# Two more tiles' own rows in the second phases, logits inside the second layer, one expert computed on all rows

## The chip, the core and the metric

The kernel runs on one core of a Trainium2 chip. The core has a matrix engine (TensorE, PE in the profile, with its weight loads as PEld), a vector engine (DVE), a scalar engine (ACT), GpSimd (POOL, which here mostly issues gathers) and a queue engine (SP, which here issues plain transfers). Each engine runs its own instructions strictly in its own order and waits on semaphores for the others. The metric is the device time of one execution in microseconds (us). Three runs of the kernel before took 981.47, 988.24 and 991.53 us; the median is 988.24.

## What is computed

1250 nodes with 512 features and 20000 edges. Two graph layers with a maximum over neighbours, then a feed-forward layer in which each of eight experts chooses 512 rows:

```
x = x + gnn(layernorm(x))          # two layers, each: relu(segment_max(x[src], dst) @ W_rel.T + b + x @ W_root.T)
y = layernorm(x)
probs = softmax(y @ Wr, axis=0)    # [N, 8], softmax over the rows
vals, idx = top_k(probs.T, 512)    # every expert picks 512 rows
h = gelu(y[idx] @ W1 + b1)         # [8, 512, 256]
x = x.at[idx].add(vals * (h @ W2 + b2))
```

All of it is in float32 to the outside.

## The kernel before, in words

Rows are held in ten tiles of 125 nodes (`acc` holds the running maximum of each tile, 512 wide). `fast_gnn` (line 42) does the two layers, `expert_choice` (line 1121) the rest. A wrapper (`InOrder`, line 24) pins every instruction of `fast_gnn` to the order in which the program writes it, and puts it on one line of the profile, L34. In `expert_choice` the engines are called without the wrapper, and the scheduler may interleave instructions of different steps.

The sources of a node are taken in three ways. Up to two sources per block of 125 source rows are picked by **blocks**: 100 steps per layer (`block_steps`, line 557), each six one-hot matmuls of 512 columns into `pq`, then one `tensor_max` of 1024 columns on DVE into `acc2`. Seven further sources per node are its **own rows** (`own`, line 451): seven gathers per tile by `nat_i`, in groups of four and three, merged on DVE (`merged`, `joined`). What is left over is **late rows** (`late_groups`, line 646): 107 gathers per layer, in 30 groups, for nodes sorted by how much they have left; their result goes to a table in memory (`late_d`, in the profile `ovf_d`) and is fetched back by one gather per tile (`backs`). A group's buffer is `hb`, of which there are four, and POOL issues every gather.

Each layer has two phases. `first_phase` (line 586) runs the blocks, spreads the merges of the gathered groups evenly between them (`due`), and lays the root product (`root_part`, line 290: four transposes, a bias matmul and four matmuls with `wroot`, stored in `root_d`) between them too. In layer 0 the own rows of tiles 0 to 2 come before the phase (`KEPT`), and those of tiles 3 to 5 at its end; in layer 1 those of tiles 0 to 5 (`EARLY = 6`). The gathers of a group are written, and so issued, ahead of the blocks that precede its merge.

`second_phase` (line 701) does the own rows that are left (tiles 6 to 9, `own_rest`), fetches the late rows back for four, four and two tiles, and finishes the tiles in order: `turn` transposes a tile, `conv` (line 670) multiplies it by `wrel` and adds the root row that SP has fetched into `ahead`, and `finish` is `hidden` in layer 0 (relu, store to the next layer's table, split in three bf16 parts by `parts`) and `residual` in layer 1 (fetch the row of x, add, moments, normalise, store to `y_d`, transpose into `yT`). A `finish` is a generator: its next stage runs when the next tile ends, so that three or four tiles are under way. `yT` lies in the memory of the one-hots (`ohs`), which are dead by then.

`expert_choice` loads the router's weights, multiplies them with `yT` in three chunks (line 1185; each router column is repeated over 16 partitions, which search different bounds at once), takes the exponent over the rows (line 1193), searches the bar of the 512th value in eight rounds of a 1250-wide count on DVE and a small matmul (lines 1233 to 1249), numbers the chosen rows by scans (1256 to 1264), adds the bias product of the experts to all rows and stores them (1268 to 1273), and turns the numbers into row lists by one-hot matmuls (`listed`, line 1295). Then each expert gathers its 512 rows (`gathered`), transposes them, multiplies by `w1` (line 1335), applies gelu, multiplies by `w2` (line 1342), scales (1345) and adds its rows to the output by indirect transfers (1346).

Of the kernel before, what the change touches and what calls it, by code (L numbers as in the profile page):

```python
# [9 lines left out]
F32 = mybir.dt.float32  # L10
# [8 lines left out]
P = 128  # L19
# [22 lines left out]
def fast_gnn(tc, ctx, sh, io, y_d):  # L42

# [223 lines left out]
    def parts(t, row, last):  # L267

        act.copy(xh[:TN, t, 0, :], row)
        yield  # L270
        dve.tensor_sub(row, row, xh[:TN, t, 0, :])
        act.copy(xh[:TN, t, 1, :], row)
        yield
        last.tensor_sub(xh[:TN, t, 2, :], row, xh[:TN, t, 1, :])
        yield
# [13 lines left out]

    def root_part(layer, t):  # L290
# [4 lines left out]
        fetch_row(layer, t + 3)  # L295
# [20 lines left out]
    def begin_rows(t0, t1):  # L316
        inverted(t0, t1)
        for t in range(t0, t1):
            normed(t, acc[:TN, t, :])
            stored(table_d[0][t * BR:t * BR + BN, :], acc[:, t, :])  # L320
            split[t] = parts(t, acc[:TN, t, :], pool)
            next(split[t])
# [134 lines left out]
    EARLY = 6  # L457
# [122 lines left out]
    ROOT_PIECES = 2 + KC  # L580

# [4 lines left out]
    def first_phase(layer, lead, groups, lists, blocks, done):  # L586
# [20 lines left out]
        for n, (rows, i, fresh, whole) in enumerate(groups):  # L607
            due = lead + (n_steps - lead) * n // len(groups)
# [54 lines left out]
    ahead = {}  # L663

    def fetch_root(layer, t):
        if t < NT:
            ahead[t] = rl = gk.tile([P, D], F32, name="ahead", bufs=4)
            sp.dma_start(rl[:TN], root_d[layer][t * TN:(t + 1) * TN, :])

# [7 lines left out]
    def hidden(t, pm):  # L677
# [4 lines left out]
        yield from parts(t, row[:TN], dve)  # L682

    def residual(t, pm):
# [13 lines left out]
        turned(yn[:TN], yT[:, :, t * TN:(t + 1) * TN])  # L698
        yield

    def second_phase(layer, finish, beside):
# [36 lines left out]
        for t in range(3):  # L738
            fetch_root(layer, t)
        order = list(range(EARLY, NT))  # L740
        own_rest(order[0])
        backs((0, 1, 2, 3))
        ready = (0, 1, 2, 3)
        ended(0, 1)
        own_rest(order[1])
        ended(2, 3)
        backs((4, 5, 6, 7))
        ready = (4, 5, 6, 7)
        ended(4, 5)
        own_rest(order[2])  # L750
        ended(6, 7)
        own_rest(order[3])
# [4 lines left out]
        while going:  # L757
            on()

    pbad = ps_m.tile([P, D], F32, name="pm")  # L760
    pe.matmul(pbad[:1, :1], bads, ones_col, start=True, stop=True)
    dve.tensor_scalar(flag_i, pbad[:1, :1], 1.0, None, op0=ALU.min)
    first_phase(0, 6, late_groups(0) + own_groups(0, range(KEPT, EARLY)), set(),
                block_steps(set(range(KEPT))), 0)
    load_root(1)
# [3 lines left out]
    def begun():  # L769
        for _ in range(2 * ready_steps):  # L770
            next(blocks)
# [4 lines left out]
    first_phase(1, 10, late_groups(1) + own_groups(1, range(EARLY)), set(range(NT)), blocks, ready_steps)  # L776
    second_phase(1, residual, lambda: None)
    gctx.close()
    return acc, yT, flag_i
# [341 lines left out]
def expert_choice(tc, ctx, sh, xs, yT, y_d, out):  # L1121
# [3 lines left out]
    ident, node_tile, rows = sh["ident"], sh["TN"], sh["rows"]  # L1125
    wr, fw1, fb1_t, fw2, fb2 = sh["wr"], sh["fw1"], sh["fb1_t"], sh["fw2"], sh["fb2"]
# [4 lines left out]
    TN = node_tile  # L1131
    NT = len(rows)
    CAP = min(512, N)
    R = P // E
    chunks = []
    step = (N + 2) // 3
    for c0 in range(0, N, step):
        chunks.append((c0, min(step, N - c0)))
    rp = ctx.enter_context(tc.tile_pool(name="route", bufs=1))
    rp2 = ctx.enter_context(tc.tile_pool(name="route2", bufs=2))  # L1140
    fwp = ctx.enter_context(tc.tile_pool(name="fwp", bufs=2))
    ps_t = ctx.enter_context(tc.tile_pool(name="fps_t", bufs=2, space=PSUM))
    ps_m = ctx.enter_context(tc.tile_pool(name="fps_m", bufs=3, space=PSUM))
    ps_x = ctx.enter_context(tc.tile_pool(name="ps_x", bufs=1, space=PSUM))


    wr_s = rp.tile([P, KC, E], F32, name="wr_s")
    nc.sync.dma_start(wr_s, wr.rearrange("(c p) e -> p c e", p=P))
    wr_rep = rp.tile([P, KC, E, R], F32, name="wr_rep")
    for c in range(KC):  # L1150
        nc.gpsimd.tensor_copy(wr_rep[:, c], wr_s[:, c].unsqueeze(2).to_broadcast([P, E, R]))
    alike = rp.tile([P, P], F32, name="alike")
    nc.gpsimd.memset(alike, 1.0)
    alike_v = alike.rearrange("p (e r) -> p e r", r=R)
# [317 lines left out]
```

## Time and profile before

The profiled execution took 982.43 us by itself; its span from the first to the last instruction is 980.7 us, at a mean granted PE clock of 0.905. It lies 5.8 us under the median of the three runs. All stage times below are of that execution.

| stage | from to (us) | length |
|---|---|---|
| loading, normalising, lists of sources | 0 to 128 | 128 |
| first phase, layer 0 | 128 to 350 | 222 |
| second phase, layer 0 | 350 to 431.5 | 81 |
| first phase, layer 1 | 431.5 to 652 | 221 |
| second phase, layer 1 | 652 to 742 | 90 |
| logits, exponent | 742 to 758.6 | 16 |
| search of the bar | 758.6 to 783.7 | 25 |
| scans, lists, first gathers | 783.7 to 830.5 | 47 |
| eight experts | 830.5 to 962 | 132 |
| last additions and end | 962 to 980.7 | 19 |

| engine | busy us | share of the span |
|---|---|---|
| PE | 685.5 | 70% |
| DVE | 668.2 | 68% |
| POOL | 527.9 | 54% |
| ACT | 143.6 | 15% |

How to read it: an engine's busy time says little about the end, because the stages have different limits. What counts is the last wait to end in each stage. In a line of the timeline the first two numbers are the start and the length, then come engine, source line, operation, output and inputs, how many instructions are merged, and in brackets how long the engine had been idle and what released it.

### The profile page before, as it was taken

What the parts mean: (1) busy time and instruction counts of PE and PEld (TensorE: products, weight loads), DVE (VectorE), ACT (ScalarE), POOL (GpSimd) and SP (SyncE); (2) the same over time, 40 slices, a digit from 0 to 9 for tenths busy, and PEclk for the clock granted to TensorE, in tenths of its full rate; (3) what the DMA queues carried; (4) which work ended last, traced back from release to release, by engine and by line L of the source; (5) the groups of instructions that cost most, each with busy time, mean ns of one, the idle gap of its engine ahead of it and who ended that gap; (6) DMA issues with size and microseconds to landing.
All of it is one profiled execution on the core that took longest, in us unless ns stands there. A gap on an engine that the chain in (4) does not pass through costs nothing.

```text
span 980.7 us, 8205 instructions
## 1 busy us (share of the span) xinstructions
PE 685.5 (70%) x2367; PEld 362.0 (37%) x2367; DVE 668.2 (68%) x1248; ACT 143.6 (15%) x259; POOL 527.9 (54%) x528
## 2 busy tenths in 40 slices
PE   0000527888989859879888898866875255999992
PEld 0000314444545424435444454432433223454440
DVE  6799649899998854728998998983543775232211
ACT  0700000000100003320000010000322001222210
POOL 6743667766667664037777777775300003464642
PEclk9999968899999979979999999987987565999996
DMA  7438477967767675337977887666623004688863
GB/s 197 124 104 235 120 213 182 220 201 213 236 208 231 178 234 196 109 114 218 205 242 219 262 261 229 203 197 213 221 82 120 1 26 167 143 200 173 192 105 46
DMA packets 71001, 172.63 MB, mean 176 GB/s; under 512 B 12887, under 2 KB 17557, under 8 KB 70947
## 3 DMA queue, kind: packets, MB, share of 16 engines
q0 software_dynamic: 38368, 116.29, 44.5%
q1 hardware_dynamic: 31598, 54.60, 17.7%
q10 hardware_dynamic: 980, 1.12, 0.5%
q8 instruction: 21, 0.34, 0.1%
q14 instruction: 34, 0.27, 0.1%
HBM read 142.48 MB, written 29.45 MB: 175 GB/s over the span
## 4 chain that ended last, share of the span: by engine, by line
PE 27%; DVE 23%; DMA 22%; POOL 12%; issue 10%; ACT 3%; SPq 1%; ACTq 0%; DVEq 0%; POOLq 0%
POOL hb L34 10%; DMA hb<-table_d,late_i 10%; PE pm L34 6%; PE pm L1335 6%; DVE acc L34 6%; PE pm L1342 5%; PE pq L34 4%; DMA line<-in_x 4%; DVE wide L34 4%; DVE hb L34 4%; DMA ahead<-root_d 2%; DVE keys L34 1%; DMA pl_i<-in_dst 1%; DMA hb<-table_d,nat_i 1%; PE pt L1329 1%
## 5 line engine op out<-in xcount | busy, mean ns | idle before, releaser
L34 PE MATMUL pq<-xh,ohs 126*125 126x512 bf16 x1200 | 297.2, 391 | 75.5 <-DVE acc L34 72.9
L34 POOL DMA_INDIRECT hb<-table_d,late_i x214 | 226.2, 1057 | 115.3 <-issue 51.7
L34 PEld LDWEIGHTS <-ohs 126*125 126x125 bf16 x1200 | 165.8, 140 | 228.5 <-issue 156.5
L34 DVE TENSOR_TENSOR acc<-acc,pq 125x1024 f32<-125x1024 f32 x180 | 219.1, 1217 | 42.6 <-PE pq L34 35.2
L34 POOL DMA_INDIRECT hb<-table_d,nat_i x140 | 147.7, 1055 | 94.4 <-issue 34.8
L34 PE MATMUL pm<-wrel,turn 128*125 128x512 f32 x160 | 82.6, 664 | 12.2 <-DVE acc L34 11.6
L1315 POOL DMA_INDIRECT ysel<-y_d,idx x32 | 30.9, 965 | 111.2 <-PE pi L1300 72.5
L34 PE MATMUL pm<-wroot,turn 128*125 128x512 f32 x160 | 87.0, 626 | 0.0
L34 ACT COPY acc<-pq 125x1024 f32<-125x1024 f32 x20 | 20.2, 1012 | 380.9 <-PE pq L34 362.7
L34 DVE TENSOR_TENSOR wide<-wide,hb 125x1024 f32<-125x1024 f32 (+1 forms) x60 | 71.4, 1190 | 1.9
L1345 DVE TENSOR_SCALAR oo<-pm,val 128x512 f32<-128x512 f32 x32 | 24.0, 751 | 62.7 <-PE pm L1342 62.7
L1346 POOL DMA_INDIRECT out<-oo,idx x32 | 50.3, 1573 | 28.0 <-DVE oo L1345 19.8
L1335 PE MATMUL pm<-yselT,w 128*128 128x512 f32 x128 | 58.0, 607 | 1.2 <-ACT yselT L1330 1.0
L1342 PE MATMUL pm<-w,hT 128*128 128x512 f32 x128 | 57.7, 599 | 0.0
L34 DVE TENSOR_TENSOR hb<-hb 125x1024 f32<-125x1024 f32 (+2 forms) x55 | 52.6, 957 | 2.3 <-DMA hb<-table_d,late_i 2.1
L34 DVE TENSOR_TENSOR wide<-hb 125x1024 f32<-125x1024 f32 (+1 forms) x40 | 48.0, 1200 | 6.6 <-DMA hb<-table_d,late_i 6.4
L34 PEld LDWEIGHTS pm<-wrel,turn 128*125 128x125 f32 x160 | 32.5, 213 | 51.5 <-issue 48.0
L34 PE MATMUL pt<-ident,loc 125*20 125x125 f32 x10 | 3.3, 386 | 61.1 <-DVE loc L34 60.7
L34 PEld LDWEIGHTS pm<-wroot,turn 128*125 128x125 f32 x160 | 32.5, 204 | 11.5 <-issue 3.1
L1342 PEld LDWEIGHTS pm<-w,hT 128*128 128x128 f32 x128 | 23.7, 190 | 32.8 <-issue 26.8
L1335 PEld LDWEIGHTS pm<-yselT,w 128*128 128x128 f32 x128 | 24.2, 194 | 29.7 <-issue 27.4
L34 POOL DMA_INDIRECT hb<-ovf_d,slot_i x20 | 19.6, 978 | 24.7 <-DVE wide L34 19.5
(222 smaller groups left out, 700.2 us busy)
## 6 DMA issues: line engine op xcount, KB each, us to landing
w<-in_fw SPq DMA_DIRECT2D x16, 512.0 KB
ohs<-idx_d SPq DMA_DIRECT2D x10, 615.2 KB
ahead<-table_d SPq DMA_DIRECT2D x20, 250.0 KB
root_d<-line SPq DMA_DIRECT2D x20, 250.0 KB
ahead<-root_d SPq DMA_DIRECT2D x20, 250.0 KB
ovf_d<-line SPq DMA_DIRECT2D x18, 224.0 KB
hb<-table_d,late_i POOLq DMA_INDIRECT x214, 6.0
line<-in_x SPq DMA_DIRECT2D x10, 250.0 KB
```

Source lines behind the costliest of these rows:

```text
L34: made = call(*args, **kwargs)
L1315: nc.gpsimd.indirect_dma_start(out=ysel[:, c, :], out_offset=None, in_=y_d[:, :], in_offset=bass.IndirectOffsetOnAxis(ap=idx[:, c:c + 1], ...
L1329: nc.tensor.transpose(pt[:, k, :], ysel[:, c, k * P:(k + 1) * P], ident)
L1335: nc.tensor.matmul(ph[:, :CAP], w1[:, k, f * P:(f + 1) * P], yselT[:, k, :], start=(k == 0), stop=(k == KC - 1))
L1342: nc.tensor.matmul(po, hT[:, f, c * P:(c + 1) * P], w2[:, f, :], start=(f == 0), stop=(f == FC - 1))
L1345: nc.vector.tensor_scalar_mul(oo, po, val[:, c:c + 1])
L1346: add = nc.gpsimd.indirect_dma_start(out=out[:, :], out_offset=bass.IndirectOffsetOnAxis(ap=idx[:, c:c + 1], axis=0), in_=oo[:, :], in_off ...
```

## The change

**Tiles.** `EARLY` goes from 6 to 4: the own rows of tiles 4 and 5 leave both first phases and go to the second phases, whose order is written out anew. `BEFORE = 4` lets four more blocks run ahead of the first merge in both first phases. The small matmul for the flag (`pbad`) moves behind the first phase of layer 0. The load of layer 1's root weights moves from before the second phase of layer 0 to just before its last two tiles. The root rows of tiles 0 to 2 are fetched from `root_part` (tiles 7 to 9) and no longer at the start of the second phase. `parts` gets a second row to write the difference to, instead of writing over the row that is being stored.

**Head.** A new function `routing_head` is called between the first and second phase of layer 1. Its small tensors and the weights of expert 0 lie in the unused rest of `ohs`. In the order of the program it puts twelve transfers on SP (the router's weights, `w1` and `w2` of expert 0 with 512 KB each, biases), and on POOL the masks, index rows and the repeated router weights, all ahead of the second phase's gathers and rows. `residual` gets a fifth stage that computes the logits of its tile, with a copy on ACT and a maximum on DVE.

**Experts.** `expert_choice` is now pinned to program order too. Expert 0 is computed on all 1250 rows (`dense_steps`: 24 matmuls of 417 columns, 20 of 512, in pieces placed between the rounds of the search and after it), and is added to the rows with a gate that is zero where the row was not chosen. The other seven experts go on as before, with three weight buffers instead of two; the list of expert e+1 is made before the work of expert e.

```diff
-    def parts(t, row, last):
+    def parts(t, row, r1, last):
         act.copy(xh[:TN, t, 0, :], row)
         yield
-        dve.tensor_sub(row, row, xh[:TN, t, 0, :])
-        act.copy(xh[:TN, t, 1, :], row)
+        dve.tensor_sub(r1, row, xh[:TN, t, 0, :])
+        act.copy(xh[:TN, t, 1, :], r1)
...
     def root_part(layer, t):
-        fetch_row(layer, t + 3)
+        if t + 3 < NT:
+            fetch_row(layer, t + 3)
+        else:
+            fetch_root(layer, t + 3 - NT)
...
-    EARLY = 6
+    EARLY = 4
+    BEFORE = 4
...
-            due = lead + (n_steps - lead) * n // len(groups)
+            due = lead + BEFORE + (n_steps - lead - BEFORE) * n // len(groups)
...
     def residual(t, pm):
...
         turned(yn[:TN], yT[:, :, t * TN:(t + 1) * TN])
         yield
+        head["logits"](t, ps_q.tile([P, R, D], F32, name="pq")[:, 0, :])
+        yield
...
-        for t in range(3):
-            fetch_root(layer, t)
-        order = list(range(EARLY, NT))
-        own_rest(order[0])
+        own_rest(4)
         backs((0, 1, 2, 3))
+        own_rest(5)
         ended(0, 1)
-        own_rest(order[1])
+        own_rest(6)
         ended(2, 3)
         backs((4, 5, 6, 7))
+        own_rest(7)
         ended(4, 5)
-        own_rest(order[2])
+        own_rest(8)
         ended(6, 7)
-        own_rest(order[3])
+        own_rest(9)
         beside()
         backs((8, 9))
         ended(8, 9)
...
-    load_root(1)
     def begun():
+        load_root(1)
         for _ in range(2 * ready_steps):
             next(blocks)
...
+    spare = ohs.rearrange("p t n -> p (t n)").bitcast(F32)[:, KC * N:]
+    head = routing_head(tc, sh, spare, yT)
     second_phase(1, residual, lambda: None)
...
+def routing_head(tc, sh, spare, yT):
+    sp.dma_start(wr_s, wr.rearrange("(c p) e -> p c e", p=P))
+    for e in range(DENSE):
+        sp.dma_start(w1, fw1[e].rearrange("(c p) f -> p c f", p=P))
+        sp.dma_start(w2, fw2[e].rearrange("(c p) d -> p c d", p=P))
+    sp.dma_start(fb1_s, fb1_t)
+    for e in range(E):
+        sp.dma_start(fb2_s[e * R:e * R + 1, :], fb2[e:e + 1, :])
...
+    for c in range(KC):
+        pool.tensor_copy(wr_rep[:, c], wr_s[:, c].unsqueeze(2).to_broadcast([P, E, R]))
+    def logits(t, pl):
+        for c in range(KC):
+            pe.matmul(pl[:, :r], wr_rep[:, c].rearrange("p e r -> p (e r)"),
+                      yT[:, c, t * TN:t * TN + r], start=(c == 0), stop=(c == KC - 1))
+        act.copy(prob[:, t * TN:t * TN + r], pl[:, :r])
+        dve.reduce_max(tops[:, t:t + 1], prob[:, t * TN:t * TN + r], axis=AX.X)
...
 def expert_choice(tc, ctx, sh, xs, yT, y_d, out, head):
+    def dense_steps():
+        for e in range(DENSE):
+            for c0, w in chunks:
+                for f in range(FC):
+                    for k in range(KC):
+                        pe.matmul(ph[:, :w], w1[:, k, f * P:(f + 1) * P], yT[:, k, c0:c0 + w], ...)
+                        if k % 2:
+                            yield
+                    act.activation(hT[f][:, c0:c0 + w], ph[:, :w], AF.Gelu, ...)
+            for t in range(NT):
+                for f in range(FC):
+                    pe.matmul(po[:r], hT[f][:, t * TN:t * TN + r], w2[:, f, :], ...)
+                act.copy(res[e][:r, t, :], po[:r])
+                yield
+    dve.reduce_max(sm[:, 0:1], head["tops"], axis=AX.X)
+    act.activation(prob, prob, AF.Exp, bias=sm[:, 1:2], accum_out=sm[:, 2:3])
+    beside(2)
...
         pe.matmul(pn, alike, sat, start=True, stop=True)
+        if i == 0:
+            by_token(prob, pcol)
+        else:
+            beside()
...
+    beside(9)
     by_token(place, at)
+    beside(4)
...
+    def own_row(t):
+        pe.matmul(po[:r], chosen[:, t * TN:t * TN + r], fb2_s, start=True, stop=True)
+        dve.tensor_add(xs[:r, t, :], xs[:r, t, :], po[:r])
+        for e in range(DENSE):
+            dve.scalar_tensor_tensor(xs[:r, t, :], res[e][:r, t, :], gate[:r, t, e:e + 1], xs[:r, t, :], ...)
+        sp.dma_start(out[t * TN:t * TN + r, :], xs[:r, t, :])
...
+    made = listed(DENSE)
+    ysel = gathered(made[0])
+    for _ in steps:
+        pass
+    for t in range(NT):
+        own_row(t)
+    for e in range(DENSE, E):
+        work = expert(e, *made, ysel)
+        if e + 1 < E:
+            nxt = listed(e + 1)
+            ysel_n = gathered(nxt[0])
+        next(work)
+        next(work)
```

## The prediction

> **What bounds the kernel now.** I read the table of windows by stage first, because every stage has its own limit, then the timeline around each boundary, then the waits. Columns: window, length, busy time (instructions) of PE, PE's weight loads, DVE, ACT, POOL, then PE's granted clock, DMA share, GB/s.
>
> ```profile
> 128.00:352.00 224.00, 180.11 (x682) 98.73 (x681) 199.70 (x236) 19.28 (x28) 150.34 (x145) 0.92 0.72 206
> 352.00:431.00 79.00, 63.36 (x176) 30.71 (x176) 38.68 (x51) 23.29 (x40) 22.90 (x23) 0.90 0.49 158
> 431.00:652.00 221.00, 186.78 (x704) 101.89 (x704) 193.94 (x184) 20.46 (x30) 171.34 (x160) 0.95 0.78 227
> 652.00:742.00 90.00, 62.07 (x180) 30.98 (x180) 45.15 (x109) 19.59 (x40) 29.20 (x35) 0.84 0.53 172
> 742.00:759.00 17.00, 10.57 (x25) 5.57 (x26) 4.25 (x16) 3.32 (x8) 0.99 (x4) 0.80 0.40 129
> 759.00:784.00 25.00, 8.16 (x26) 6.09 (x25) 18.63 (x60) 1.65 (x10) 0.00 (x0) 0.50 0.00 1
> 784.00:830.00 46.00, 22.41 (x88) 13.72 (x89) 32.85 (x91) 3.59 (x14) 7.68 (x8) 0.61 0.29 99
> 830.00:962.00 132.00, 129.41 (x408) 62.37 (x406) 33.13 (x88) 28.12 (x46) 70.65 (x55) 0.99 0.72 154
> ```
>
> The first phases are DVE's (199.7 of 224 us, 193.9 of 221), with PE at 180 to 187. The second phases are no engine's: PE 62 of 90, DVE 45, POOL 29; they are waits. The search leaves PE idle, and the experts are PE's (129.4 of 132).
>
> The timeline shows which waits (start, length, engine, operation, in brackets the idle time before it and what ended it):
>
> ```profile
> 138.98 1.23 DVE L34 TENSOR_TENSOR wide<-hb 125x1024 f32<-125x1024 f32 x1 [5.72 <-DMA hb<-table_d,late_i]
> ...
> 367.39 1.12 PE L34 MATMUL pm<-ahead,ident 125*125 125x512 f32 x2 [4.30 <-DMA ahead<-root_d]
> ...
> 431.49 0.94 POOL L34 DMA_INDIRECT hb<-table_d,late_i  x1 [30.80 <-DVE line L34]
> ...
> 654.51 1.43 SPq L34 DMA_DIRECT2D line<-in_x  x1
> ...
> 677.97 0.69 DVE L34 SCALAR_TENSOR_TENSOR acc<-pm,line 125x512 f32<-125x512 f32 x1 [18.85 <-DMA line<-in_x]
> ...
> 744.07 10.28 PE L1185 MATMUL pm<-ohs,wr_rep 128*128 128x417 f32 x24 [2.52 <-POOL wr_rep L1151]
> ...
> 744.31 1.28 ACT L1193 ACT_TABLE_LOAD   x1 [2.15 <-DMA fb_s<-in_fb]
> ...
> 947.94 7.13 PE L1335 MATMUL pm<-yselT,w 128*128 128x512 f32 x16 [0.68 <-ACT yselT L1330]
> ```
>
> Read from these: the first merge of layer 0 waits 5.7 us for a gather; POOL stands still for 30.8 us of the second phase of layer 0; in layer 1 the row of `x` issued at 654.51 is used only at 677.97: SP moved about 1.0 MB in 25.8 us (39.7 GB/s) while POOL issued a 250 KB gather every 1.25 us (200 GB/s).
>
> **The change part by part**, as time after less time before.
>
> (a) First phase, layer 0: **-10**. An own tile's merges are five DVE operations, 1.22 + 0.69 + 1.23 + 0.69 + 0.69 = 4.5 us; two tiles, 9.0. Four more blocks ahead fill some 3 of the 5.7 us (a block is six matmuls, 1.4 us on PE, and 1.22 on DVE). PE, 180 us with a further wait behind each block, gives 2 back. Bounds: -15 (9.0 + 5.7, all paid) to -5.
>
> (b) Second phase, layer 0: **-5**. Added: 14 gathers at 0.95 + 0.30 us on POOL, 17.5 us, under its 30.8 us idle, and 9.0 us of DVE, which is busy 38.7 of 79. Gone: the 4.3 us wait for the first root row, and the waits of the in-place subtraction for the store of the same row (DVE waits 25.2 us in seven places for `table_d<-line`, most of them hidden). What is late next is the gathers. Bounds: -9 (4.3 + one uncovered wait of about 5) to +4 (half of the merges uncovered).
>
> (c) First phase, layer 1: **-8**. Again 9.0 of DVE, and 14 gathers less (about 19 of POOL's 171). No wait stands at its start to be filled; PE, at 187 of 221, keeps 1. Bounds: -15 (POOL's relief paid too, where its buffers hold blocks up) to -2 (PE and the gathers already bind).
>
> (d) Second phase, layer 1: **+21**. In the changed order the four copies of the repeated router weights stand on POOL ahead of all gathers of this phase and wait for SP's transfer of `wr`, which stands behind the last store of `root_d`, at the phase's start. Before, 11 gathers (own rows of tile 6, four late ones) were issued in the 15 us ahead of it. The same transfer and copies took 2.2 + 1.0 us at 741.58 to 744.7, so the first gather is issued some 3.4 us into the phase. Tile 4's product needs the 29th gather (7 + 4 + 7 + 7 + 4): 3.4 + 29 x 1.25 + 6.3 for landing (as for the late rows before) + 4 for merge, transposes and copy = 50 us into the phase; before it began at 692.3, 40.1 in: +10. From there on each tile's step gets four logits matmuls (10.28 us for 1250 rows, 1.03 a tile), a copy on ACT (0.58) and a maximum on DVE, which stands ahead of the addition that frees the next product's PSUM; DVE's merges (4.5) come into the same step. Steps were 5.3 to 6.7 us apart undisturbed; I take 7.9. Tile 4's product to the last copy of `yT`: 5 x 7.9 + 12.5 (as before, 729.7 to 742.2) + three logits stages with nothing beside them (1.03 + 0.58 + 0.25 + four handovers of 0.35 = 3.3 each) = 62, against 49.9: +12, of which I count 11. Bounds: +12 (steps at 6.7, half the drain hidden) to +28 (steps at 9).
>
> (e) From the last copy of `yT` to the search: **-9**. Before, 16.4 us: transfer, copies, 10.28 of matmuls, exponent. After: one tile's logits 1.9, handovers 1, maximum over tiles 0.5, and the exponent with its table load, 4: 7.4. Before, the table load (1.28 us at 744.31) ran under the matmuls; in the changed order it follows the last copy of logits and carries DVE's wait, so it counts. Bounds -11 to -7.
>
> The Trainium skill ("ScalarE: Activation LUTs", section "What ACT_TABLE_LOAD costs") agrees on the load, 1283 ns, but adds a drain of some 1380 ns, 2.66 us a switch; by it (e) would be -7.6. The rows show the load alone.
>
> (f) Search and scans: **+1**. The pieces of the dense expert lie between rounds of 3.15 us in which PE worked 8.2 of 25 us; seven fewer small DVE operations (0.19 each) speak for, its transposes (1.6 us) in front of the scans' matmuls against. Bounds -2 to +3.
>
> (g) Lists and experts: **+3**. Before, 34.3 us from the last scan to the first expert matmul, and eight periods of 16.63. The dense expert takes one period out, -16.6. Against it: its gated rows, 10 x 2 x 0.69 = 14 us on DVE between the first list and the second; the lists of expert e+2, ten one-hots and matmuls, stand on PE ahead of expert e+1's transposes, and their one-hots behind expert e's last four scalings. So a boundary between experts is some 6.0 us, not 2.43: four scalings 3.0 + ten one-hots 1.7 + matmul and handovers 1.3. Start +2; experts: 7 x (7.13 + 7.05) = 99.3, + 5 x 6.0 + one of 3.1 = 132.4 against 131.6. Sum +2.7. Bounds: -15 (lists stay hidden, boundaries at 2.43) to +7.
>
> Sum: -10 - 5 - 8 + 21 - 9 + 1 + 3 = **-7**: 982.4 becomes 975.4. The profiled execution lies 5.8 under the median of the runs, so the median becomes 981.
>
> **The rivals.**
>
> *A, clearly faster.* The first phases pay in full and one of the two givers-back does not give back: -14 - 8 - 13 + 16 - 9 + 0 + 0 = -28, so 954 of the profile's time, 960 on the median. For it: DVE has 90% of the first phases; the sum of the removed work (18 in the first phases, 9 at the logits, 16.6 of an expert) is 43 us. Against: PE at 85% is right behind DVE, and the printed order shows the lists in front. It covers 960 to 978.
>
> *B, slower: SP starves behind the head's weights.* 1.06 MB of `w1`, `w2` and router weights stand on SP ahead of the rows of `x`, while 52 gathers stream for 65 us without a break. At the 39.7 GB/s that SP had under gathers, a tile's two rows (some 500 KB) take 12.9 us; the step needs them in 7.9. Four tiles then lose 5 each, and the weights' own passage adds some 2: +22 to the sum, 1003 on the median. It decides from the point where SP's share stays under 500 KB / 7.9 us = 65 GB/s until tile 4. For it: the 18.85 us wait above. Against: gathers pause when their four buffers are full, and then SP has the rest.
>
> The Trainium skill ("DMA: Bandwidth & Descriptors", section "Queues, rings and completion order") has each DMA engine serve its queues in turn, packet by packet. Read as equal shares, SP would get about 100 GB/s and B would not happen; the row shows 39.7, so B stays.
>
> *C, the dense expert does not shorten the path.* It is in the forecast (-16.6, given back by +14 on DVE and five longer boundaries). If the lists are hidden after all, (g) is -15 and the total lies in A.
>
> **How the numbers follow.** A measurement of this kernel can tell about 1% (9.9 us) from no change; the runs shown spread 981.5 to 991.5. Forecast, within 1%: 0.42. A: 0.36, since it needs only two of (a), (c), (d), (g) at their better ends. Slower: 0.22, mostly B (0.15), the rest (d) and (g) both at their worse ends (+28 and +7 make the sum +4, so this needs (a) or (c) to fail as well, 0.07). The range goes from 958, short of A's full price, to 1003, B's; about 1 in 10 is left out at each end.
>
> **What would show it.** First phases of about 212 and 213 us; second phase of layer 0 about 76. In the second phase of layer 1 (about 111): the router copies idle for `wr_s` ahead of the first gather, tile 4's product 50 us in, DVE's maximum waiting for ACT's copy. Exponent within 4 us of the last logits; PE's clock near full in the search, where it was 0.50. Some 14 us of gated rows on DVE between the first two lists; 6 us between the last `w2` matmul of an expert and the first `w1` matmul of the next, five times. Wrong if: additions of `x` wait over 10 us for SP in several tiles (B), boundaries stay at 2.4 (A), or the first phases keep their length, PE having become the limit.

## The result, and the profile after

The changed kernel takes **987.95 us** (median of 20 runs, 980.93 to 990.46), the kernel before in the same sittings 987.66 (20 runs, 981.47 to 996.68). The ratio is **0.9994, with a 95% interval of 0.997 to 1.0019**: no difference. In a second sitting it was 1.0032 (0.9992 to 1.0072). Forecast was 981, 0.7% less, "within 1%" as the likeliest case.

The profiled execution took 990.10 us, its span is 988.0. Its stage table, with the same columns as the one of before (PE, weight loads, DVE, ACT, POOL, granted clock, DMA share, GB/s):

```profile
128.00:341.00 213.00, 179.28 (x684) 98.55 (x683) 191.54 (x229) 19.27 (x28) 137.31 (x132) 0.93 0.72 204
341.00:417.00 76.00, 63.10 (x176) 30.44 (x176) 46.20 (x59) 22.70 (x40) 38.40 (x37) 0.89 0.63 198
417.00:631.00 214.00, 183.29 (x704) 100.44 (x704) 186.64 (x176) 20.81 (x31) 142.30 (x142) 0.97 0.71 210
631.00:755.00 124.00, 73.29 (x255) 40.46 (x256) 56.51 (x127) 22.39 (x49) 54.07 (x56) 0.79 0.58 177
755.00:761.00 6.00, 3.83 (x15) 2.01 (x14) 1.97 (x10) 2.98 (x4) 0.00 (x0) 1.00 0.66 224
761.00:784.00 23.00, 17.78 (x54) 9.78 (x55) 17.04 (x55) 5.31 (x15) 0.00 (x0) 0.85 0.09 34
784.00:832.00 48.00, 39.89 (x121) 19.59 (x120) 37.16 (x78) 10.64 (x26) 6.85 (x8) 0.93 0.20 64
832.00:970.00 138.00, 126.15 (x370) 60.53 (x369) 32.62 (x98) 22.99 (x38) 61.76 (x48) 0.94 0.62 136
```

Both first phases are shorter (213 and 214 us, where 224 and 221 stood), and so are the logits and the search. The fourth row has it all back: the second phase of layer 1 takes 124 us where it took 90, with no engine busier than 60%. The timeline shows what it waits for, in order of time:

```profile
419.37 0.94 POOL L34 DMA_INDIRECT hb<-table_d,late_i  x1 [29.00 <-DVE line L34]
...
630.25 0.25 SPq L34 DMA_DIRECT2D root_d<-line  x1
630.55 0.40 SPq L34 DMA_DIRECT2D ohs<-in_wr  x1
...
635.73 0.99 POOL L34 COPY ohs<-ohs 128x128 f32<-128x128 f32 x4 [22.59 <-DMA ohs<-in_wr]
636.88 1.02 POOL L34 DMA_INDIRECT hb<-table_d,nat_i  x1 [0.16 <-issue]
...
648.56 1.23 DVE L34 TENSOR_TENSOR wide<-hb 125x1024 f32<-125x1024 f32 x1 [15.23 <-DMA hb<-table_d,nat_i]
...
712.77 0.69 DVE L34 SCALAR_TENSOR_TENSOR acc<-pm,line 125x512 f32<-125x512 f32 x1 [2.91 <-DMA line<-in_x]
...
721.95 0.28 DVE L34 TENSOR_REDUCE ohs<-ohs 128x1 f32<-128x125 f32 x1 [7.36 <-ACT ohs L34]
...
739.36 0.28 DVE L34 TENSOR_REDUCE ohs<-ohs 128x1 f32<-128x125 f32 x1 [9.35 <-ACT ohs L34]
...
756.85 1.28 ACT L34 ACT_TABLE_LOAD   x1 [0.78 <-DVE sm L34]
758.14 1.34 ACT L34 ACTIVATE ohs<-ohs,sm 128x1250 f32<-128x1250 f32 x1
```

POOL stands still for 22.6 us in front of the copies of the router's weights, whose transfer stands on SP behind the store of the last root row and is issued only at 630.55. The first gather follows at 636.88, and DVE waits 15.2 us for the rows of the first gathers. Later DVE waits 7.4 and 9.4 us in front of the maximum of a tile's logits (TENSOR_REDUCE), with the addition that frees the next product's PSUM behind it. The row of `x`, which cost 18.85 us before, is late by 2.9 us once.

Single profiles scatter, so the stages are compared over three profiles of before and two of after, all from sittings in which before took 986 to 993 us. "Last block" is the start of the last matmul of a layer's blocks; the second phase of layer 0 is counted up to the end of the tenth block of layer 1 (the start of the eleventh), since the first ten run beside it.

| stage (us) | forecast | before | after | difference |
|---|---|---|---|---|
| (a) to the last block, layer 0 | -10 | 349.5 | 336.8 | -12.7 |
| (b) to the tenth block, layer 1 | -5 | 101.3 | 99.7 | -1.6 |
| (c) to the last block, layer 1 | -8 | 203.0 | 192.7 | -10.3 |
| (d) to the last copy of `yT` | +21 | 91.4 | 125.4 | **+34.0** |
| (e) to the search | -9 | 16.3 | 6.7 | -9.6 |
| (f) to the end of the scans | +1 | 37.6 | 35.2 | -2.4 |
| (g) to the end | +3 | 185.4 | 190.5 | +5.1 |
| sum | -7 | 984.5 | 987.0 | +2.5 |

The last sum agrees with the ratios (0.9994 and 1.0032). Three profiles of before end at 980.7, 985.4 and 987.4 us; most of that scatter (650, 656, 655) is there at the last block of layer 1.

### The profile page after: what moved, and what is told of

Same layout as the page of the kernel before. It is cut to its first block, busy times and chain, and to the rows that moved or that the text cites. A ratio compares the mean times of both kernels' runs of the same rounds, so it can differ in the third digit from the quotient of the medians.

```text
span 988.0 us, 8381 instructions
## 1 busy us (share of the span) xinstructions
PE 711.6 (72%) x2453; PEld 374.9 (38%) x2453; DVE 671.0 (68%) x1246; ACT 151.4 (15%) x275; POOL 513.9 (52%) x520
## 3 DMA queue, kind: packets, MB, share of 16 engines
q1 hardware_dynamic: 31758, 54.63, 17.5%
## 4 chain that ended last, share of the span: by engine, by line
PE 33%; DVE 24%; DMA 15%; POOL 11%; issue 11%; ACT 3%; SPq 0%; ACTq 0%; DVEq 0%; POOLq 0%
PE pm L34 19%; PE pq L34 9%; POOL hb L34 9%; DVE acc L34 7%; DMA hb<-table_d,late_i 5%; DVE wide L34 5%; DMA hb<-table_d,nat_i 4%; DVE hb L34 4%; PE pt L34 3%; DMA line<-in_x 2%; DMA pl_i<-in_dst 1%; DVE keys L34 1%; POOL rest_d L34 1%; POOL out L34 1%; DVE jk L34 1%
## 5 line engine op out<-in xcount | busy, mean ns | idle before, releaser
L34 PE MATMUL pq<-xh,ohs 126*125 126x512 bf16 x1200 | 298.0, 393 | 64.1 <-DVE acc L34 62.4
L34 POOL DMA_INDIRECT hb<-table_d,nat_i x140 | 143.7, 1026 | 67.5 <-issue 35.5
L34 PE MATMUL pm<-wrel,turn 128*125 128x512 f32 x160 | 85.1, 681 | 17.9 <-DVE acc L34 14.2
L34 DVE TENSOR_SCALAR oo<-pm,val 128x512 f32<-128x512 f32 x28 | 21.0, 751 | 107.4 <-PE pm L34 107.4
L34 POOL DMA_INDIRECT ysel<-y_d,idx x28 | 27.1, 967 | 125.5 <-PE pm L34 103.1
L34 POOL DMA_INDIRECT out<-oo,idx x28 | 44.1, 1576 | 67.7 <-DVE oo L34 49.8
L34 ACT COPY acc<-pq 125x1024 f32<-125x1024 f32 x20 | 20.2, 1012 | 360.9 <-PE pq L34 360.9
L34 DVE TENSOR_TENSOR hb<-hb 125x1024 f32<-125x1024 f32 (+2 forms) x55 | 52.7, 958 | 18.3 <-DMA hb<-table_d,nat_i 18.3
L34 PE MATMUL pm<-yselT,w 128*128 128x512 f32 x112 | 52.4, 623 | 4.7 <-ACT yselT L34 4.7
L34 PE MATMUL pm<-w,hT 128*128 128x512 f32 x112 | 50.5, 599 | 0.0
L34 PE MATMUL pt<-ident,acc 125*128 125x125 f32 x80 | 14.2, 321 | 42.2 <-DVE acc L34 42.0
L34 ACT COPY turn<-pt 128x500 f32<-128x500 f32 x40 | 22.7, 574 | 77.8 <-PE pt L34 77.8
L34 PEld LDWEIGHTS pm<-yselT,w 128*128 128x128 f32 x112 | 21.6, 198 | 31.8 <-issue 25.0
```

Source lines behind the costliest of these rows:

```text
L34: made = call(*args, **kwargs)
```

## The experiments

The runs were made in five sittings. In two of them the kernel before took 1028 and 1032 us, so a ratio is to before in the same sitting, and stage times are compared only between like sittings.

**1. Which part costs, which part gains.** The change of the tiles alone (`fast_gnn` as changed, without the fifth stage of `residual` and `routing_head`; the old `expert_choice`), and the head and the experts alone:

```diff
-        head["logits"](t, ps_q.tile([P, R, D], F32, name="pq")[:, 0, :])
-        yield
...
-    head = routing_head(tc, sh, spare, yT)
```

> The kernel before with the change of the tiles alone: own rows of tiles 4 and 5 in the second phases, four blocks ahead, root rows from the root product, the second row for the split. Logits, exponent, search, scans and experts are those of before. Theory: the 34 us that the second phase of layer 1 grew by are mostly the head's, because no gather is issued before the router's weights are there. Without the head the gathers of tile 4 are issued among the last blocks, the first product starts some 10 us after the last block (29 in the changed kernel), the phase grows by 8 to 12 us for 14 more gathers and 9.0 us of merges, the first phases keep the 21 us that they won, and the whole is 10 to 13 us under the kernel before (ratio 0.987 to 0.990). Rival: the own rows of two more tiles themselves cost the phase 25 us or more, then the whole is within 4 us of before.

```diff
-    EARLY = 4
-    BEFORE = 4
+    EARLY = 6
+    BEFORE = 0
...
-        own_rest(4)
+        own_rest(6)
         backs((0, 1, 2, 3))
-        own_rest(5)
         ended(0, 1)
-        own_rest(6)
+        own_rest(7)
...
```

> The changed kernel with the order of the tiles and the number of early own rows as before (six tiles early, no blocks ahead): head, logits in the layer, dense expert and lists as changed. Theory: first phases as before; the first gather of the second phase of layer 1 waits for the router's weights, so the first product starts some 25 us after the last block and the phase grows by 20 to 25 us; from the last transpose to the first expert 11 us less, experts 6 us more: 15 to 20 us over the kernel before (ratio 1.015 to 1.020). Rival, the own rows are what costs: the phase grows by no more than 8, and the whole is 3 us over or under before.

Measured: tiles alone **0.9796** (0.9749 to 0.9843), head alone **1.0078** (1.003 to 1.0126). With the tiles alone the first product of layer 1's second phase starts 9.3 us after the last block, as before; with the head alone 29.3 us, as in the changed kernel. So the late start is the head's, and the change is a gain from the tiles and a loss from the head. The gain was larger than I expected, and the loss smaller (0.8%, where 1.5 to 2.0% was forecast). The two do not make up the changed kernel between them: 0.9796 x 1.0078 is 0.987, and it measured 0.9994 and 1.0032 elsewhere. It was not run in this sitting, and whether the rest belongs to the two parts together or to the sitting is not shown.

**2. What delays the first gather.** The head's POOL instructions, and the DVE instructions that use them, are put into a function that is called later:

```diff
+    def small():
+        pool.memset(alike, 1.0)
...
+        for c in range(KC):
+            pool.tensor_copy(wr_rep[:, c], wr_s[:, c].unsqueeze(2).to_broadcast([P, E, R]))
...
         own_rest(6)
+        small()
         ended(2, 3)
```

> The changed kernel, but what the head puts on POOL (masks, index rows, the repeated router weights) and the DVE instructions that use it are written after the own rows of tile 6, and no longer ahead of the first gather; the head's transfers on SP stay where they are. Theory: gathers go out among the last blocks again, the first product starts some 10 us after the last block instead of 29, tile 4's at about 42 instead of 61, and all that follows comes 15 to 19 us earlier (ratio to before about 0.982). Rival one: SP is then the limit, because 1.06 MB of weights stand ahead of the rows of x while gathers stream; the first product comes earlier, but additions of x wait 10 us and more and the end moves by 5 us or less. Rival two: the steps of the tiles themselves (7 to 8 us each) are the limit and the first product's start is caught up later; also 5 us or less.

Measured: **0.9811** (0.9762 to 0.9861). The first product starts 10.0 us after the last block, and the phase is 107.5 us long, against 124 with the head alone (six early tiles) in the same sitting. Rival one has a part in it, as the waits of DVE in this phase show (what waits for what: us in all, times, longest):

```profile
DVE ohs L34 <- ACT ohs L34: 22.4, 7, 8.1
DVE acc L34 <- DMA line<-in_x: 15.2, 2, 8.5
```

The rows of `x` are 15.2 us late in two waits, and the maximum's wait stays. The changed kernel was not run in this sitting; experiment 4 has it beside the kernel with this and the next edit.

**3. The lists between the experts.**

```diff
-            oh = rp2.tile([P, P], BF16, name="oh", bufs=4)
+            oh = rp2.tile([P, P], BF16, name="oh", bufs=10)
...
         work = expert(e, *made, ysel)
+        next(work)
         if e + 1 < E:
             nxt = listed(e + 1)
             ysel_n = gathered(nxt[0])
         next(work)
-        next(work)
```

> The changed kernel, but the list of the next expert (ten one-hots on DVE, ten matmuls, the gathers) is written between the first and the second product of the expert before it, and ten one-hots may be alive at once instead of four. Theory: the lists cost PE some 1 us inside the expert and no longer stand between the last scaling and the next transposes; a period of the experts goes from 21.1 to 17 us, five times, and the first expert no longer waits for the second list behind the gated rows on DVE (some 5 us): 23 to 28 us under the changed kernel, ratio to before 0.972 to 0.977. Rival: the time between experts is the transposes at a low clock and the landing of the gathered rows, not the lists; then the period stays above 19 us and the gain is under 12.

Measured: **0.9895** (0.9823 to 0.9967), a smaller gain than forecast. In the stages it is there: the way from the last scan to the first expert takes 27.8 us instead of the 35.7 of the kernel with the masks later in the same sitting, and the experts 124.0 instead of 136.4, 20.3 together; a period is 18.3 on the mean, not 17. The changed kernel was not run in this sitting, whose second phase of layer 1 was long (135 us), so the total is no clean test. The next sitting has one.

**4. Both mends, and the rows of `x` first.** The first of these two kernels has both edits above. The second also moves the transfers of `w1` and `w2` of expert 0 and of the biases into a function that is called behind the last tile, so that only `wr` stays ahead:

```diff
         ended(8, 9)
+        loads()
```

> The changed kernel itself, to have it beside the others on one chip and to see how its stages scatter. Theory: the total lies within 0.5% of before (it was 0.9994), and the last block of layer 1 comes some 25 us sooner than before, the second phase of layer 1 is 30 to 35 us longer, from the last transpose to the first expert 11 us shorter, the experts 6 us longer. Rival: the gain of the first phases was a lucky execution; then the last block comes less than 15 us sooner and the total is 1% or more over before.

> The kernel before itself, profiled on the same chip: the stages scatter by some 5 us up to the last block of layer 1 and by 2 us or less in each later stage. If the later stages scatter as much as the first phases, the differences of the stages read from single profiles are worth less than I take them for.

> The changed kernel with the head's POOL and DVE instructions after the own rows of tile 6, and with the next expert's list between the two products of the expert before (ten one-hots alive). Theory: the two gains lie in stages one after the other and add up: 18 us from the second phase of layer 1 and 20 us from the experts' start and periods, 35 to 40 us under the changed kernel. Rival: the earlier gathers leave SP less, the additions of x wait for their rows, and the sum is below 28.

> As the one with both edits, but the transfers of w1, w2 and the biases of expert 0 (1.06 MB on SP) stand behind the last row of x, and only the router's weights (16 KB) stay at the head. Theory: if the rows of x wait for the weights (15 us in two waits in the one with the masks later), the second phase of layer 1 is another 8 to 12 us shorter. Rival: the waits are for the gathers, which take the bandwidth whatever stands on SP; then it is within 3 us of the one with both edits.

Measured: the changed kernel 1.0032 (0.9992 to 1.0072), the kernel before against itself 1.0032 (0.9991 to 1.0073), both mends **0.9595** (0.9533 to 0.9656), rows first **0.9579** (0.9517 to 0.9641). Both mends take 42 us from the changed kernel (988.3 to 946.6). The stages of the two profiles of this sitting show both gains: the second phase of layer 1 takes 104.0 us instead of 124.7, the way from the search to the first expert 63.1 instead of 70.8, and the experts 121.7 instead of 135.1. POOL now gathers while the blocks still run (the last block is at 628.0), and PE makes the list between the two products of an expert:

```profile
621.20 0.95 POOL L34 DMA_INDIRECT hb<-ovf_d,slot_i  x1 [0.30 <-DVE acc L34]
...
801.25 7.13 PE L34 MATMUL pm<-yselT,w 128*128 128x512 f32 x16 [0.67 <-ACT yselT L34]
808.22 0.40 PE L34 MATMUL pi<-pays,oh 128*128 128x20 bf16 x10
808.47 7.11 PE L34 MATMUL pm<-w,hT 128*128 128x512 f32 x16
```

By 621.20 the own rows of tile 4 have all been issued. With both mends the rows of `x` are late by only 3.9 us in two waits of this phase, although the weights stand ahead of them as in the run with the 15.2. Rows first takes this to 0.4 and shortens the phase from 104.0 to 99.1 us (8 to 12 were forecast), but its total is the same within the intervals: its experts took 6 us longer at a lower clock. So 5 us are seen in a stage and not in a total.

**5. The logits inside the layer.** In both kernels on top of rows first:

```diff
-        dve.reduce_max(tops[:, t:t + 1], prob[:, t * TN:t * TN + r], axis=AX.X)
...
-    dve.reduce_max(sm[:, 0:1], head["tops"], axis=AX.X)
+    dve.reduce_max(sm[:, 0:1], prob, axis=AX.X)
```

> The kernel with masks later, lists inside and the rows first, as run already, to stand beside the next two on one chip. Theory: ratio to before again 0.955 to 0.965; the second phase of layer 1 about 99 us from the last block to the last transpose. If the ratio lies outside of this, the scatter between executions is larger than the intervals say.

> As the one before (rows first), but the maximum of each tile's logits on DVE is left out of the layer, and one maximum over all 1250 columns is taken after the last copy (1.5 us on DVE). Theory: the maximum stands ahead of the addition that frees the next product's PSUM and waits there for PE and ACT (7.36 us in the longest case of the changed kernel); without it the phase is 6 to 10 us shorter from tile 4's product on, the exponent starts 1.3 us later after the last transpose, and the whole gains 5 to 9 us. Rival: PE's logits matmuls in front of the next product, or the gathers of the last two tiles, set the step; then the gain is under 2 us or a loss of 1.

```diff
-        head["logits"](t, ps_q.tile([P, R, D], F32, name="pq")[:, 0, :])
-        yield
...
+    for t in range(NT):
+        head["logits"](t, ps_q.tile([P, R, D], F32, name="pq")[:, 0, :])
```

> As rows first, but the logits of all ten tiles (matmuls, copies, maxima) are made after the last transpose, and no longer inside the second phase. Theory: what the logits inside the layer cost there (some 10 us in the second half of the phase) is about what they save behind it (10 us from the last transpose to the search): the phase is 8 to 11 us shorter, the way to the search 9 to 12 us longer, and the whole stays within 3 us. Rival: the phase's second half is the gathers' and not the logits'; then the phase keeps its length and the whole is 8 to 12 us longer.

Measured, in a sitting in which before took 1032 us: rows first again 0.9873 (0.98 to 0.9945), which is outside of what I expected and shows that a ratio does not carry from one sitting to another; one maximum 0.9804 (0.9728 to 0.988); logits after 0.9782 (0.9728 to 0.9835). The phase takes 112.6, 100.6 and 97.8 us, the way to the search 6.2, 7.2 and 14.5. The intervals of the totals overlap; the stages say that with the maximum in the tile's step the logits cost 14.8 us in the layer and save 8.3 behind it, and that the maximum by itself is 12.0 of the 14.8. This 12.0 is from one profiled execution that took 993.5 us, the fastest of its four (median 1003.9), so it may be too large. That the two would balance within 3 us was forecast; by the medians logits after is 0.9% better, which the intervals leave open.

To see the same in the changed kernel, the maximum alone was moved there, and all mends were put together (with no blocks ahead, see below):

> The changed kernel with the maximum alone moved behind the layer. Theory: tile 4's product stays where it is (59 us after the last block), from there to the last transpose 8 to 12 us less than the 62 to 65 of the changed kernel, the exponent 1 us later; ratio to before 0.990 to 0.994 where the changed kernel has 0.999 to 1.003. Rival: the gathers of the last two tiles, late by the late start, set the end of the phase; then less than 3 us.

> Masks later, lists inside, rows first, one maximum behind the layer, and no blocks ahead: all mends together. On a chip that takes 987 us for the kernel before: 946 for the first three, less 7 for the maximum, less 0 to 3 for the blocks, 936 to 940 (ratio 0.947 to 0.953); on one that takes 1030, ratio 0.965 to 0.98. Rival: the maximum was worth 12 us only because that chip's rows came late; then 0.955 to 0.96 on the quicker chip.

Measured: maximum alone **0.9916** (0.9884 to 0.9948), all mends **0.9493** (0.9441 to 0.9545), 938.78 us against 988.69, which beats both kernels and lies in the range that was expected. With the maximum moved, tile 4's product stays where it was (61.0 us after the last block, 61.3 in the changed kernel), and from there to the last copy of `yT` it takes 56.9 instead of 64.1 us: a gain of 7, a little less than I expected.

**6. What gains in the tiles.** The small edits alone are the kernel before with the flag's matmul moved, the root rows fetched from `root_part`, the later load of the root weights and the second row in `parts`. Then come the own rows with the new order (`EARLY` is 4), without and with blocks ahead (`BEFORE` is 0, then 4). The small edits alone against the complete change of the tiles, with the old order of the second phases:

```diff
-    EARLY = 4
+    EARLY = 6
...
-    BEFORE = 4
+    BEFORE = 0
```

> The changed kernel with no blocks ahead of the first merge (as before the change in this one point). Theory by my sum: the four blocks ahead are worth about 3 us in layer 0, where they fill a wait of 5.7 us, and nothing in layer 1; 2 to 4 us over the changed kernel. Rival: they shift all merges later and starve nothing; then no difference within 2 us, and the whole gain of the first phases is the own rows'.

> The kernel before, profiled on the chip on which the next three run: the last block of layer 0 some 348, of layer 1 some 650 to 655 us after the start on a chip that takes 987 us for it, or 20 to 40 us later on one that takes 1030.

> The kernel before with the small edits alone: the flag's matmul behind the first phase, root rows of tiles 0 to 2 fetched from the root product, the load of the root weights later, and the split written to a second row. Six early tiles and no blocks ahead, as before. Theory by my sum: only the 4.3 us wait for the root row and one wait of the split, 4 to 6 us under before in the second phase of layer 0 and nothing elsewhere. Rival: these edits are worth most of the 23 us: 12 us or more under before at the last block of layer 1.

> The small edits and four early tiles with the new order of the second phases, but no blocks ahead. Theory by my sum: 9 us per first phase under the small edits alone, of which the second phase of layer 0 takes nothing back and that of layer 1 takes 6 back: 12 us under it in all. Rival: the second phases take the 18 us back (14 us in layer 0), and it stays within 4 us of the small edits alone.

> The change of the tiles complete, with four blocks ahead. Theory: 2 to 4 us under the one with no blocks ahead, from the 5.7 us wait before the first merge of layer 0. Rival: no difference within 2 us, or some us over it, as the first phase of layer 0 was shorter without blocks ahead in the changed kernel (341 against 348 to 354 us at its last block on one chip).

Measured: the changed kernel with no blocks ahead 1.007 (1.0017 to 1.0122) in the sitting of 1032 us, where the changed kernel was not run beside it; then, in one sitting, small edits **0.98** (0.9736 to 0.9865), own rows too 0.9743 (0.9677 to 0.9808), blocks ahead too 0.9738 (0.9672 to 0.9803). Most of the gain is the small edits', some 20 us where 4 to 6 were forecast; by the medians the own rows add 6 us (12 were forecast) and the blocks ahead nothing. Which of the four small edits is worth how much was not run. The waits of the second phase of layer 0, first of the small edits alone, then with the own rows:

```profile
DVE xh L34 <- ACT xh L34: 12.1, 4, 5.6
DVE line L34 <- ACT xh L34: 8.1, 1, 8.1
```

```profile
DVE hb L34 <- DMA hb<-table_d,nat_i: 14.1, 4, 5.8
```

The waits of DVE for the store of its own row (19.2 us in the profile of before of this sitting) are gone with the small edits, and what waits in their place is the split by ACT. With the own rows DVE waits for the landing of gathers, in order, ahead of the late rows of the tiles that are to be finished.

The stages side by side, from the sittings near 988 us (lengths in us; "product" is that of a tile with `wrel` in layer 1):

| kernel | last block L0 | tenth block L1 | last block L1 | first product | tile 4's product | last `yT` | search | first expert | last `w2` |
|---|---|---|---|---|---|---|---|---|---|
| before (3) | 349.5 | 101.3 | 203.0 | 9.3 | 32.5 | 49.7 | 16.3 | 72.1 | 131.4 |
| small edits | 347.8 | 91.5 | 201.5 | 9.3 | 26.1 | 50.0 | 17.6 | 73.4 | 131.5 |
| + own rows | 335.6 | 102.0 | 188.8 | 9.3 | 25.4 | 59.2 | 16.3 | 73.9 | 130.6 |
| + blocks ahead | 337.9 | 100.4 | 192.7 | 9.3 | 28.0 | 58.4 | 16.3 | 74.1 | 130.9 |
| changed (2) | 336.8 | 99.7 | 192.7 | 29.7 | 31.6 | 64.1 | 6.7 | 70.9 | 136.6 |
| all mended | 339.6 | 100.0 | 191.4 | 9.8 | 28.9 | 57.1 | 7.2 | 63.0 | 122.6 |

## Why the prediction was right and wrong

The sum was some 10 us off (-7 against +2.5 in the profiles), and the step that failed is **(d), the second phase of layer 1: +34.0 where I said +21**, outside its own bounds of +12 to +28. That the total still fell within 1% of before, the case held likeliest, is in part luck: several terms were off by about 10 us, in both directions.

- *The late first gather*, said to be worth +10 at tile 4's product, was worth +19.5 there. The mechanism was right, and the mend shows it: without the copies ahead of the gathers the first product is back at 9.8 us. Two things in the term were wrong. I took the transfer of `wr` at the 2.2 us of before and had the first gather 3.4 us into the phase; counted in the same way (the phase of before started at 652.14, 2.3 us after its last block) it comes at 6.2. And I let the 29th gather decide where tile 4's product lies, as if the four tiles ahead of it would be through by then. The gathers themselves ran as I had counted (the 29th is issued at 673.12, 36.2 us after the first); with my 6.3 and 4 us behind it, tile 4's product would have started at 683.4, but it starts at 689.53. The tiles ahead of it are not through: the first product waits for the merges of tile 4's own rows, which stand ahead of the late rows on DVE, and starts 20 us late; the four steps then take what they always took (31.6 us, 32.5 before). A delay at the head of a row of dependent steps moves all of them.
- *The tile's step*, said to be worth +11, was worth +14.4 (49.7 to 64.1). By the table the own rows are some 9 of it (58.4 and 59.2 without the head), and by the experiment the maximum in front of the addition is 7. I had named both, but the two sizes that I added up were wrong in opposite directions. A step between the products of tiles 4 to 9 took 10.2 and 9.6 us on the mean of the two profiles, not 7.9. I had started from the undisturbed 5.3 to 6.7 us of before, but its five steps have one of 12.3 among them and a mean of 7.5. And from tile 9's product to the last copy of `yT` it took 13.9 and 15.1 us, not the 12.5 + 9.9 = 22.4 of the sum. So the steps were some 10 us too short in the forecast and the end some 8 too long.

**(a) to (c)** came out as -24.6 where -23 was forecast, but not by my steps. The own rows take 12.2 us from the first phase of layer 0 and 12.7 from that of layer 1, more than the 9.0 of merges, and they give 10.5 back in the second phase of layer 0, which I had at nothing, "under POOL's 30.8 us idle". POOL was indeed free; the landing of the gathers, in DVE's order, was not. The small edits, which I had at -5 with the root row's 4.3 us as the main item, are worth 9.8 there and 6 in layer 1, where the root rows no longer stand on SP ahead of the first row of `x` (the waits of DVE for these rows go from 28.4 to 18.3 us); on the whole kernel they are the 2.0% of the ratio 0.98. The four blocks ahead are worth nothing that the runs show: -3 was forecast, and the total is the same with and without them. Errors of about 10 us cancelled here, by luck.

**(e)** was right (-9.6 against -9): the exponent's table load is on the chain and costs its own 1.28 us. The page "ScalarE: Activation LUTs" of the Trainium skill, in its section "What ACT_TABLE_LOAD costs", adds a drain of some 1380 ns; the exponent here starts 0.01 us after the load ends (756.85 + 1.28 to 758.14), so no drain is seen behind this load and the row decides.

**(f)** was off by 3.4 us to the good. A round of the search went from 3.15 to 2.57 us. I had priced one small operation less; the matmul beside full PE work also takes 0.42 us from its input to the next operation instead of 0.63 (granted clock 0.85 instead of 0.50), and the adding of the bits is no longer on the chain.

**(g)** was right in kind. A period of the experts is 20.2 us in the undisturbed ones, as forecast (7.13 + 7.05 + 6.0), and the list in front of the transposes is the cause, since with both mends, where it is moved, the last four periods are 17.4 to 17.5 (the first two 19.1 and 18.6). The rest is TensorE's clock, which I had not counted: the periods of the two profiles lie 5.6 and 2.7 us in all over the forecast, and each one that does has a group of transposes or a first product that ran at a lower clock (see below).

Of the rivals, **B** (SP starves) did not come, for a reason that I had not seen: the same wait that holds POOL for 22.6 us leaves SP alone with the weights, at 196 GB/s between 630.5 and 637. When the gathers go first, rows of `x` are late by 15.2 us in two waits in one run and by 3.9 in two in another (both mends), with the weights in the same place; with all mends and the weights behind the rows, it is 9.9 us in three. So it is not shown that the weights are what makes them late. The price of B was also too high: my 39.7 GB/s counted only four transfers of 250 KB up to the row that was waited for, while SP's queue moved 1.42 MB between 654 and 678 us of before (lines below), 59 GB/s. At that rate a tile's two rows take 8.7 us, not 12.9. **A** is what the mended kernels are; for the changed kernel both givers-back gave back. **C** was in the forecast and is so: the dense expert takes one period of 16.6 us out, but the seven others take 136.6 us where eight took 131.4, and the first of them starts only 1.2 us sooner behind the search.

## What to carry to other kernels

An instruction that is put into an in-order queue at a phase's border costs what the queue would have done *before* the border too: look at how far ahead of the border the first work of the phase was issued, not only at how long the new wait lasts. A small operation that waits for two other engines must not stand ahead of the one that frees a buffer for the next step; one maximum in place of ten was worth 7 us. And a sum that comes out right does not show that its terms are: only taking the parts of a change one by one did.

## What was not expected of the hardware

- **The transfer of 16 KB took 5.2 us instead of 2.2** (issued at 630.55, used at 635.73; before, 741.58 to 743.73). It is 5.2 us in the second profile of the changed kernel, the head alone and the lists inside too. Two transfers of 512 KB stand right behind it; that these slow it was not tested.
- **TensorE's clock between experts.** The wait for the lists leaves PE idle for a microsecond or two, and now and then the granted clock falls from 1.00 to 0.50 for part of the next expert (between 890 and 899 us, for one). In that boundary of the changed kernel the first nine matmuls of an expert took 6.4 us; in the next, sixteen took 7.1 (columns: window, length, PE, loads, DVE, ACT, POOL, clock, DMA share, GB/s):

```profile
894.00:901.00 7.00, 6.35 (x9) 2.74 (x10) 0.00 (x0) 0.63 (x2) 1.89 (x2) 0.59 0.51 157
915.00:924.00 9.00, 8.03 (x27) 3.90 (x26) 0.00 (x0) 2.75 (x5) 3.88 (x4) 1.00 0.75 185
```

  The sixteen transposes ahead of an expert took 3.59 us in such a case and 2.51 in an undisturbed one of the same execution. The Trainium skill ("TensorE: Matmul & The Clock Gate", section "What's actually happening") gives windows of some 3.4 us in which the gate decides; here the loss comes in some boundaries and not in others of one execution, though PE waits 1.01 and then 0.3 us for the one-hots ahead of both of the two shown. With it go some 3 to 6 us of the experts' stage.
- **SP under gathers.** The two queues moved (packets, MB, share of the 16 engines), first between 654 and 678 us of before, then between 637 and 663 us of the changed kernel, then in the same stretch of the kernel with all mends:

```profile
q0 software_dynamic: 1242, 4.05, 54.0%
q1 hardware_dynamic: 716, 1.42, 17.9%
...
q0 software_dynamic: 1493, 4.92, 64.4%
q1 hardware_dynamic: 471, 0.84, 9.8%
...
q0 software_dynamic: 1318, 4.35, 57.5%
q1 hardware_dynamic: 991, 1.63, 18.4%
```

  The 0.84 MB of the changed kernel, 32 GB/s, are not what gathers leave to SP: it issues three transfers of 250 KB between 639 and 640 us and the next only at 663.81. With all mends it moves 63 GB/s beside the gathers. The Trainium skill ("DMA: Bandwidth & Descriptors", section "Queues, rings and completion order") has each DMA engine serve its queues in turn, packet by packet; here the plain queue moved 716 and 991 packets beside 1242 and 1318 of the gathers, and whether both had work all the time is not shown.
- **Sittings.** The kernel before took 986 to 993 us in three sittings and 1028 and 1032 in two. By the two profiles of rows first the added time lay in the phases that gather, and rows first was worth 4.2% in one sitting and 1.3% in another. The record has the same chip number for the first sitting (1028 us) and the last (989), so the chip alone does not decide it. The cause stays open.
